# Two attention blocks on one core: the fifth product of the single-product pair placed ahead of the second

## The chip, the cores and the metric

The kernel runs on one core of a Trainium2 chip. The metric is the device time of one execution in microseconds. A core has a matrix engine (TensorE, in the profile PE for the matmuls and PEld for the loads of their stationary operand), three engines for elementwise work (VectorE or DVE, ScalarE or ACT, GpSimd or POOL) and a queue that issues transfers (SyncE or SP). Each engine works through its own list of instructions in order.[...]

## The reference

Two attention blocks follow one another on an input of 8 images, each 512 channels by 1024 positions, all in fp32:

```python
# block 0: 8 heads of 64 channels
h = group_norm(x, gn_weight, gn_bias)                       # 32 groups
qkv = jnp.einsum('oc,bct->bot', w_qkv, h.reshape(B, C, T)) + b_qkv[None, :, None]
weight = softmax(einsum('bct,bcs->bts', q * scale, k * scale))
a = jnp.einsum('bts,bcs->bct', weight, v).reshape(B, C, T)
x = x + (jnp.einsum('oc,bct->bot', w_proj, a) + b_proj[None, :, None]).reshape(B, C, H, W)
# block 1: one head of 512 channels
xn = group_norm(x, gamma, beta)                             # 8 groups
q, k, v = conv1x1(xn, q_w, q_b), conv1x1(xn, k_w, k_b), conv1x1(xn, v_w, v_b)
attn = softmax(einsum('bqc,bck->bqk', q, k) * C**-0.5)
x = x + conv1x1(einsum('bqk,bkc->bqc', attn, v), p_w, p_b)
```

Each projection ("convolution" in the kernel's words) is a product of a 512 x 512 weight matrix with a 512 x 1024 image.

## The kernel before, in words

The kernel goes through the 8 images one after another. For an image it makes values, keys and queries of block 0 (`values`, `keys_and_queries`), the attention of block 0 with its exponentials (`attention0`), the projection of block 0 (`projection2`), and for block 1 the product that stands for queries and keys together (`layer1_scores`, name g), the scores (`scores1`), the values with the projection folded in (name z) and their weighted sums (`values1`). Block 1 of one image stands between the attention and the values of block 0 of later ones.

**A twice divided convolution.** Most projections go through `conv2` (line 536). It uses a scheme of Strassen's kind: a product of matrices cut into 2 x 2 quarters is made from seven products of sums of quarters instead of eight. `conv2` does this twice, one level inside the other. The outer level has products 1 to 7. They are made in four pairs by `pair`: first pair 0 with the outer products 1 and 5, then pair 1 with 2 and 6, then pair 2 with the single product 7, and last pair 3 with 3 and 4. Pair 2 and pair 3 are interwoven. There are 44 such convolutions: v, k, q and p seven times each, g and z eight times each.

**The steps of one pair.** Inside a pair the inner level has seven products again, and `inner_steps` (line 452) sets their order. Each is a step: matmuls into one of three accumulation banks of PSUM called a, b and c, then an addition that takes the result away. `step(1)` fills bank a, and ScalarE copies it into bank b (line 482). Step 2 adds into a, steps 6, 7 and 4 add into b one after another, and steps 5 and 3 share bank c. The additions that empty them are:

- step 6: the sum in b is read into a small tile u2 (VectorE, `put`, line 468, which calls `add`, the profile's line 566); in pair 2 one addition that pair 1 left over (`flush`) follows it;
- step 2: the sum in a goes to the quarter (0,0) of the output;
- step 5: the content of c goes to a small tile c5;
- step 7: the sum in b plus c5 goes to the quarter (1,1);
- step 3: the content of c plus u2 goes to the quarter (0,1). Its first matmul starts the bank's second use: it adds onto what step 5 left there, so it may not run before the addition of step 5 has read c;
- step 4: the sum in b goes to the quarter (1,0).

For the single product of pair 2 GpSimd adds each finished quarter to other outputs (`extra`, which calls `more`, line 571): one addition when a quarter of `x` was read, one when the quarter was written, both after the VectorE addition of that step.

**The order around the change.** Each pair runs step 1, then what the pair before left for later (its steps 3 and 4 and its closing work, through `finish`), then a list of steps. Pair 2 also runs the first step of pair 3 inside its own list (`between`). Pair 3 then runs its own list, into which the steps 3 and 4 of pair 2 are set (`order`, where -3 and -4 stand for them). The order of the matmuls is the program's: the helper `matmul` (line 59) pins each of them. Most instructions on VectorE, ScalarE and GpSimd are not pinned to a place; a planner with costs of its own puts them in order per engine when the program is built, earliest ready first, in the program's order otherwise. Callables from a list of background work are run one per step (`run_background(1)`), and lists called `hooks` are run after the steps of a pair: in the convolution k the small matmuls of a group norm (`gvar`) follow step 7 of pair 2, in z the matmuls that add up the softmax's denominators (`sums`).

PSUM: during the convolutions each of the banks a, b and c has two buffers, so consecutive pairs alternate between them. The small tiles u2 and c5 have one buffer for even and one for odd pairs (line 177, `upool`).

Of the kernel before, what the change touches and what calls it, by code (L numbers as in the profile page):

```python
# [29 lines left out]
def two_attention_blocks_kernel(  # L30
# [143 lines left out]
    def main_path(ctx):  # L174
# [42 lines left out]
        def run_background(n):  # L217
            for _ in range(min(n, len(background))):
                background.pop(0)()
# [5 lines left out]
        def finish():  # L225
            while tail:
                tail.pop(0)()
# [135 lines left out]
        def image_factors(h, uid, sub=nc.vector.tensor_sub):  # L363

            tiles = [pair_tile(f"t{i}_{uid}") for i in (1, 2, 4)]
            halves = lambda t: (t[:, :HT], t[:, HT:])
            return right_sums(
                [halves(t) for t in h[:2]], [halves(t) for t in h[2:]],
                [lambda j, t=t: t[:, j, :] for t in tiles], sub,
            )  # L370
# [81 lines left out]
        def inner_steps(uid, parity, k, mm, add, y, x, extra, after7, final, early=(), defer=None, flush=None, between=(), order=None):  # L452

            ps, tmp = {}, {}

            def bank(n):
                ps[n] = ps_pools["abc".index(n)].tile([P, 2, 2 * P], F32, tag="ps", name=f"ps{n}_{uid}")[:, :k, :]

            def keep_tmp(what, tag):
                tmp[what] = upool.tile([P, 2, 2 * P], F32, tag=f"{tag}{parity}", name=f"{what}_{uid}")[:, :k, :]
                return tmp[what]

            def put(dst, n, at):

                if x is None:  # L470
                    (d,) = dst
                    nc.scalar.copy(d, ps[n])  # L472
                else:
                    add(dst, ps[n], x(*at))

            def step(j):
                if j == 1:
                    bank("a")
                    mm(ps["a"], 1, True)

                    bank("b")
                    nc.scalar.copy(ps["b"], ps["a"])  # L482
                elif j == 6:
                    mm(ps["b"], 6, False)
                    put([keep_tmp("u2", "u")], "b", (0, 1))
                    while flush:
                        flush.pop(0)()
                    extra(0, 1, True, False)
                elif j == 2:
                    mm(ps["a"], 2, False)  # L490
                    put(y(0, 0), "a", (0, 0))
                    extra(0, 0, True, True)
                elif j == 5:
                    bank("c")
                    mm(ps["c"], 5, True)
                    put([keep_tmp("c5", "w")], "c", (1, 1))
                    extra(1, 1, True, False)
                elif j == 7:
                    mm(ps["b"], 7, False)
                    add(y(1, 1), ps["b"], [tmp["c5"]])  # L500
                    extra(1, 1, False, True)
                elif j == 3:
                    mm(ps["c"], 3, False)
                    add(y(0, 1), ps["c"], [tmp["u2"]])
                    extra(0, 1, False, True)
                elif j == 4:
                    mm(ps["b"], 4, False)
                    if defer is None:
                        put(y(1, 0), "b", (1, 0))
                    else:  # L510
                        add(y(1, 0), ps["b"], x(1, 0), (0,))
                        defer.append(lambda: add(y(1, 0), ps["b"], x(1, 0), (1,)))
                    extra(1, 0, True, True)
                run_background(1)

            def run():
                if order is None:
                    step(1)
                    finish()
                    steps = [6, 2, *between, 5, 7]  # L520
                else:
                    three, four, *rest = tail
                    tail.clear()
                    steps = [{-3: three, -4: four}.get(j, j) for j in order] + rest
                for g in early:
                    g()
                for j in steps:
                    j() if callable(j) else step(j)
                for g in after7:
                    g()  # L530
                tail.extend([lambda: step(3), lambda: step(4)])
                tail.extend(final)

            return step, run
# [641 lines left out]
        for b in range(B):  # L1176
# [19 lines left out]
            af, steps = image_factors(a, f"a_{b}", here)  # L1196
# [68 lines left out]
        hf, steps = image_factors(h, f"h1_{B - 1}")  # L1265
# [206 lines left out]
```

## Time and profile before

| what | value |
|---|---|
| median of 3 runs | 2781.55 us (2780.86 to 2782.15) |
| the profiled execution | 2781.39 us |
| its span | 2779.6 us |
| TensorE matmuls, busy | 2764.8 us |
| VectorE, busy | 2052.0 us |
| GpSimd, busy | 1297.5 us |
| ScalarE, busy | 1000.3 us |
| granted TensorE clock | 1.000 |

Busy means that an instruction of the engine was under way. Matmuls overlap in the engine and the ends of their records are modelled, so that two matmuls started 0.22 us apart each have a record of 0.38 us. Whether TensorE lost time is therefore read from the starts of successive matmuls and not from the busy share. Each fp32 matmul of the source appears as two matmul instructions with 128 x 128 stationary values; the steps of the single-product pair have one source matmul with 256 columns (or two with 128 in the convolutions by tokens, v and z), the steps of the other pairs twice that. In the profile psa_g, psb_g and psc_g are the banks of convolution g, and so for the others; u_g is the tile u2, c_g the tile c5.

### The profile page before, as it was taken

The numbers are of one execution on the slowest core, as the hardware profiler recorded it, in microseconds if no ns is written. First come the engines' busy times: TensorE is split into PE (matmuls) and PEld (weight loads), VectorE is DVE, ScalarE is ACT, GpSimd is POOL, SyncE is SP. The second block draws the span as 40 slices with busy tenths as digits, with TensorE's granted clock in tenths as the row PEclk, the third lists the DMA queues.
The fourth block names the chain that finished last, engine by engine and source line by source line (L and its number), as shares of the span: only waits on it lengthen the run. The fifth ranks groups of instructions, "written<-read, shape, count | busy, mean of one in ns | idle before, by whom it ended". The sixth has DMA issues, their size and how long they took to land.

```text
span 2779.6 us, 36877 instructions
## 1 busy us (share of the span) xinstructions
PE 2764.8 (99%) x13436; PEld 1761.6 (63%) x13436; DVE 2052.0 (74%) x3214; ACT 1000.3 (36%) x1307; POOL 1297.5 (47%) x1384
## 2 busy tenths in 40 slices
PE   9999999999999999999999999999999999999999
PEld 6437636776376853868538694486844868338585
DVE  6587777777777777777786867777678776787776
ACT  1253463214632146312463125531255312633130
POOL 2313605745067440774307752176621766136763
PEclk9999999999999999999999999999999999999999
DMA  7827412344113440144401443014521145112302
GB/s 264 251 90 251 180 32 70 138 161 162 40 62 138 169 162 32 63 163 163 149 24 63 175 178 122 32 55 183 189 104 44 62 152 209 64 50 100 141 24 74
DMA packets 126070, 332.60 MB, mean 120 GB/s; under 512 B 19831, under 2 KB 64695, under 8 KB 114362
## 3 DMA queue, kind: packets, MB, share of 16 engines
q1 hardware_dynamic: 125294, 329.75, 33.3%
q8 instruction: 108, 1.77, 0.3%
q14 instruction: 80, 0.66, 0.1%
q10 hardware_dynamic: 588, 0.42, 0.0%
HBM read 258.14 MB, written 71.99 MB: 119 GB/s over the span
## 4 chain that ended last, share of the span: by engine, by line
PE 97%; DVE 2%; DMA 0%; issue 0%; ACT 0%; SPq 0%; DVEq 0%
PE sc L60 16%; PE av L60 16%; PE psb_av L60 5%; PE psb L60 5%; PE psa_av L60 4%; PE psc_av L60 4%; PE psc L60 4%; PE psa L60 3%; PE psb_k L60 3%; PE psb_z L60 3%; PE psb_q L60 3%; PE psb_p L60 3%; PE psb_g L60 3%; PE psb_v L60 3%; PE psc_v L60 2%; PE psc_p L60 2%
## 5 line engine op out<-in xcount | busy, mean ns | idle before, releaser
L700 DVE TENSOR_TENSOR sum<-sum,e 128x1024 f32<-128x1024 f32 x384 | 473.9, 1234 | 35.9 <-DVE sum L700 0.9
L696 ACT ACTIVATE e<-sc 128x1024 f32<-128x1024 f32 x512 | 476.1, 1050 | 63.4 <-PE sc L60 62.9
L60 PE MATMUL sc<-q,k 64*128 64x512 f32 x2048 | 456.8, 596 | 0.0
L60 PE MATMUL av<-e,v 128*64 128x512 f32 x2048 | 453.4, 595 | 0.0
L60 PEld LDWEIGHTS sc<-q,k 64*128 64x128 f32 x2048 | 190.1, 185 | 246.0 <-ACT e L696 120.9
L60 PEld LDWEIGHTS av<-e,v 128*64 128x64 f32 x2048 | 141.4, 137 | 299.0 <-issue 287.9
L434 POOL TENSOR_TENSOR inner_h<-x 128x256 f32<-128x256 f32 x16 | 14.8, 924 | 415.8 <-DVE x L1028 415.8
L698 DVE TENSOR_TENSOR sum<-e,e 128x1024 f32<-128x1024 f32 x64 | 79.9, 1249 | 103.9 <-ACT e L696 103.9
L719 ACT COPY a<-av 128x512 f32<-128x512 f32 x64 | 37.6, 587 | 318.7 <-PE av L60 279.2
L126 POOL TENSOR_TENSOR rstd<-ve,mhalf 128x4 f32<-128x4 f32 x16 | 16.7, 1042 | 274.5 <-DVE ve L124 274.5
L60 PE MATMUL psb<-inner,inner_h 128*128 128x256 f32 x448 | 115.6, 380 | 0.0
L60 PE MATMUL psa_av<-e,z 128*128 128x512 f32 x256 | 112.5, 592 | 0.0
L482 ACT COPY psb_v<-psa_v 128x512 f32<-128x512 f32 (+1 forms) x28 | 14.5, 517 | 234.0 <-DVE x L845 178.1
L60 PEld LDWEIGHTS psb<-inner,inner_h 128*128 128x128 f32 x448 | 84.5, 190 | 13.6 <-POOL inner L449 1.8
L60 PE MATMUL psb_z<-w_z,inner_h 128*128 128x128 f32 x672 | 87.5, 276 | 0.1
L60 PE MATMUL psb_g<-inner_h,w_m 128*128 128x256 f32 x336 | 84.9, 381 | 0.0
L776 ACT ACTIVATE e<-e 128x1024 f32<-128x1024 f32 x64 | 65.3, 1052 | 47.0 <-DVE e L766 25.7
L60 PEld LDWEIGHTS psb_z<-w_z,inner_h 128*128 128x128 f32 x672 | 81.4, 192 | 0.8 <-ACT u_z L472 0.3
L60 PEld LDWEIGHTS psa_av<-e,z 128*128 128x128 f32 x256 | 47.4, 190 | 53.6 <-issue 51.7
L771 POOL TENSOR_TENSOR e<-e,e 128x512 f32<-128x512 f32 x64 | 79.4, 1273 | 2.2 <-DVE e L766 2.1
L482 ACT COPY psb<-psa 128x512 f32<-128x512 f32 x56 | 31.9, 570 | 130.2 <-PE psa L60 130.2
L571 POOL TENSOR_TENSOR v<-v,v 128x256 f32<-128x256 f32 x28 | 20.4, 727 | 125.0 <-DVE u_v L566 121.8
(443 smaller groups left out, 6192.5 us busy)
## 6 DMA issues: line engine op xcount, KB each, us to landing
r<-all_rows SPq DMA_DIRECT2D x78, 256.0 KB
x<-in_x SPq DMA_DIRECT2D x36, 512.0 KB
h<-in_x SPq DMA_DIRECT2D x32, 512.0 KB
spill<-x SPq DMA_DIRECT2D x32, 512.0 KB
x<-spill SPq DMA_DIRECT2D x32, 512.0 KB
out<-x SPq DMA_DIRECT2D x63, 256.0 KB
kept<-a SPq DMA_DIRECT2D x28, 512.0 KB
again<-kept SPq DMA_DIRECT2D x28, 512.0 KB
```

Of the source, the lines that this page charges most:

```text
L60: tc.keep_in_program_order(nc.tensor.matmul(*args, **kw))
L126: nc.gpsimd.tensor_tensor(rstd, ve, mhalf, ALU.pow)
L434: pin(engine.tensor_tensor(dst, x, y, ALU.subtract))
L482: nc.scalar.copy(ps["b"], ps["a"])
L571: nc.gpsimd.tensor_tensor(d, x, y, ALU.add)
L696: nc.scalar.activation(e, sc, AF.Exp, scale=(C // 8) ** -0.5)
L698: nc.vector.tensor_add(total, es[0], e)
L700: nc.vector.tensor_add(total, total, e)
L719: nc.scalar.copy(dst, av)
L771: nc.gpsimd.tensor_tensor(blocks(dst, r, cc)[0], blocks(x, r, cc)[0], blocks(y, r, cc)[0], ALU.add)
L776: nc.scalar.activation(e[c, cc, r], e[c, cc, r], AF.Exp, scale=scale)
```

## The change

One line in `inner_steps` is different:

```diff
                 if order is None:
                     step(1)
                     finish()
-                    steps = [6, 2, *between, 5, 7]
+                    steps = [6, 5, *between, 2, 7] if between else [6, 2, 5, 7]
                 else:
                     three, four, *rest = tail
                     tail.clear()
```

Only pair 2 of a `conv2` has something in `between`, namely the first step of pair 3. With A for that step, the list of pair 2 was 6, 2, A, 5, 7 and becomes 6, 5, A, 2, 7. What follows is as it was: step 3 of pair 2, step 6 of pair 3, then step 4 of pair 2 and steps 2, 5 and 7 of pair 3 (in p: 5 of pair 3, 4 of pair 2, 7 and 2 of pair 3). The steps 5 and 2 change places together with their additions on VectorE and GpSimd. No instruction is added or removed, and no buffer changes.

## The prediction

> **What bounds the kernel now.** I read the page first: TensorE is busy for 99% of the span, and the chain that ended last is 97% TensorE.
>
> ```profile
> PE 2764.8 (99%) x13436; PEld 1761.6 (63%) x13436; DVE 2052.0 (74%) x3214; ACT 1000.3 (36%) x1307; POOL 1297.5 (47%) x1384
> ...
> PE 97%; DVE 2%; DMA 0%; issue 0%; ACT 0%; SPq 0%; DVEq 0%
> ```
>
> So a time saved on TensorE counts, unless another engine takes it back. Next I asked for the waits of TensorE's weight loader, because a stopped matmul shows first at the load in front of it:
>
> ```profile
> PEld psc_g L60 <- DVE c_g L566: 3.9, 8, 0.5
> ...
> PEld psc_q L60 <- DVE c_q L566: 3.4, 7, 0.5
> PEld psc_p L60 <- DVE c_p L566: 3.4, 7, 0.5
> ...
> PEld psb_k L60 <- DVE k L566: 2.3, 7, 0.3
> PEld psc_v L60 <- DVE c_v L566: 2.2, 8, 0.4
> ...
> PEld psc_k L60 <- DVE c_k L566: 0.5, 1, 0.5
> ```
>
> A wait of bank c for the tile c5 (total, times, longest), once per convolution: 8 times in g, 7 in q and p (v has one more elsewhere). The chain, cut out at one convolution g, shows that this wait is on the path:
>
> ```profile
> 1474.34 0.45 PE psc_g L60 x2
> 1474.78 0.02 issue
> 1474.81 0.43 DVE c_g L566
> 1475.24 0.04 issue
> 1475.29 0.70 PE psc_g L60 x2
> ```
>
> This is step 5 of pair 2, its addition into c5, and step 3 of pair 2. Only step 7 stands between. Its timeline:
>
> ```profile
> 1474.17 0.59 PE L60 MATMUL psc_g<-inner_h,w_m 128*128 128x256 f32 x2
> ...
> 1474.61 0.59 PE L60 MATMUL psb_g<-inner_h,w_m 128*128 128x256 f32 x2
> ...
> 1475.28 0.30 PEld L60 LDWEIGHTS psc_g<-x,w_m 128*128 128x128 f32 x2 [0.49 <-DVE c_g L566]
> 1475.29 0.70 PE L60 MATMUL psc_g<-x,w_m 128*128 128x256 f32 x2
> 1475.34 0.42 DVE L566 TENSOR_TENSOR g<-psb_g,c_g 128x256 f32<-128x256 f32 x1
> ...
> 1475.82 0.59 PE L60 MATMUL psb_g<-inner_h,w_m 128*128 128x256 f32 x2
> ```
>
> Steps 5, 7, 3 and the next step 6 begin at 1474.17, 1474.61, 1475.29 and 1475.82. At full pace a step of two matmuls takes 0.43 (5 to 7: 0.44). Step 7 to 3 takes 0.68, 0.25 too long: the wait. Step 3 to 6 takes 0.53, 0.10 too long: the load could not run ahead (the two matmuls have 0.70 instead of 0.59). Together 0.35 us per convolution. The starts of steps 5, 7, 3, 6 in q (1313.91, 1314.34, 1315.02, 1315.56) and p (1335.41, 1335.84, 1336.52, 1337.06) give the same, and one by one all 22 in g, q and p are within 0.002 of 0.353. In v (1270.25, 1270.70, 1271.38, 1271.93, a step there 0.447) it is (0.68 - 0.447) + (0.55 - 0.447) = 0.336.
>
> **What the Trainium skill says.** "Perfetto Trace Analysis", section Tensor Engine Instruction: the recorded end of a matmul is computed, and its semaphore goes out only when PSUM has acknowledged the write. Agreed: step 5's second matmul started at 1474.39 and its record ends at 1474.77; the addition starts at 1474.81. The same page, section Matmuls: independent groups should rotate through PSUM banks so that emptying one overlaps the next matmuls. Steps 5 and 3 accumulate in one bank, so here only the steps between them can cover the emptying. "TensorE: Matmul & The Clock Gate", section Step-by-step: loads are pulled ahead of running matmuls. Agreed: a load normally starts 0.21 before its matmul; after the wait both start together (1475.28, 1475.29), which is where the extra 0.10 comes from. "SBUF — State Buffer", section SBUF: two separate sides: VectorE and GpSimd share a port pair that one holds at a time. This case's trace agrees in k: a subtraction on two SBUF inputs takes 0.67 us in one place and 1.25 beside GpSimd additions.
>
> **The change part by part.** No instruction is added or removed, no transfer is issued or passed by a moved step (neither step 5 nor 2 issues one), and background work is run one piece per step as before.
>
> *Step 5 leaves its place before 7.* The chain from step 5's last start to step 3's load is 1474.39 to 1475.28, 0.89 us. Before, 0.43 us passed from that start until step 3's load was due (0.22 to the end of the matmul's turn, 0.43 of step 7, less the 0.21 by which a load runs ahead): 0.46 too little, of which the load's lead hides 0.21. After, A (four matmuls, 0.86), 2 and 7 (0.43 each) stand between: 1.72 in place of 0.43, so the chain ends 0.8 us before the load is due. The wait goes, and with it the refill: 0.35 in g, q, p, 0.336 in v. Step 5's factor is ready: step 6, which runs first, already needs the sum made after it. Its bank buffer and c5 were last used by pair 0.
>
> *Step 2 moves behind A.* Bank a of pair 2 isn't refilled in this convolution, so no matmul waits for its addition. Two things get later. On VectorE the addition of step 2 comes right before that of step 7: 1474.81 to 1475.23 in g, then step 7's to about 1475.7, at the time where it ends now. Step 4 needs that one (bank b), and comes 0.35 earlier: its load would be due at 1476.47 - 0.35 = 1476.12, some 0.4 after. No wait, but the cover shrinks from 0.7. On GpSimd the additions of step 2 follow that of step 5; the second one, which pair 3's step 2 needs, would end near 1476.8 in place of 1475.8 (each 0.73). That step's addition on VectorE starts at 1478.60 now, 1478.25 then: 1.4 us spare. GpSimd's last addition stays near 1479.75, as it waits in between; what uses it, the factors for the scores on GpSimd, has 1.0 us to spare, 0.6 then.
>
> *Step 6 of pair 3* needs ScalarE's copy of A: 1474.38 to 1474.95 in g, unmoved; its load will be due near 1475.25. Covered by 0.3.
>
> *z.* After step 7 come the 8 matmuls of `sums`; the c5 addition (1539.62 to 1540.04) is over when step 3's load starts at 1540.53. The remaining 0.2 there follows `sums` elsewhere too. Gain 0, though the wait view names c_z.
>
> *k.* Here the planner put a subtraction between the additions of steps 5 and 7, and step 4 waits for the latter:
>
> ```profile
> 1292.84 0.42 DVE L566 TENSOR_TENSOR c_k<-psc_k,k 128x256 f32<-128x256 f32 x1 [0.64 <-PE psc_k L60]
> ...
> 1293.18 1.25 DVE L168 TENSOR_TENSOR t_a<-again 128x512 f32<-128x512 f32 x1
> ...
> 1294.35 0.41 DVE L566 TENSOR_TENSOR k<-psb_k,c_k 128x256 f32<-128x256 f32 x1
> ...
> 1294.81 0.30 PEld L60 LDWEIGHTS psb_k<-inner_h,w_k 128*128 128x128 f32 x2 [0.34 <-DVE k L566]
> ```
>
> The stall before step 3 is about 0.27 (`gvar` covers a little), that before step 4 is 0.20. If the subtraction stays at the same time, step 3's gain is lost at step 4: 0. If it moves into the new pause after c5 or behind step 7's addition, both go: 0.47. If it lands before step 7's addition and delays GpSimd as well, k may lose up to 0.5. The trace doesn't show which; I take 0.15, between the ends, nearer to no gain because both ends of that stall hang on the same subtraction.
>
> **Sum.** 22 x 0.352 (g, q, p) = 7.74; v 7 x 0.336 = 2.35; k 7 x 0.15 = 1.05 (from -3.5 to 3.3); z 0. Together 11.1 us, against the profiled execution: 2781.39 - 11.1 = 2770.3 (span 2779.6 to 2768.5, 1.8 around it unchanged). The median of the runs lies 0.16 higher: 2770.4 us, 0.40% faster.
>
> **Rivals.** (1) *The wait moves to step 4.* Step 7's addition now queues behind step 2's, while step 4 comes earlier. If VectorE is 0.4 late in each convolution, the wait starts to return; 0.75 late, and all 0.35 is gone: about 2781, no change. Against it: in g, q, v and p no other VectorE work lies in the stretch from step 6 of pair 2 to step 4; for it: k shows the form. (2) *Only part arrives*: k loses 0.5 each, or the planner, whose order is made anew for the whole program, sets a few other instructions worse: 11.1 - 4.5 = 6.6 down to 5, so 2775 to 2776.5. (3) *More arrives*: k gives all, 13.4 in all: 2768.1. (4) *Slower: GpSimd holds up pair 3.* Its addition for step 2 of pair 3 waits on VectorE for GpSimd's additions of the moved step 2. They have 1.4 us to spare, and another 0.4 until step 3 of pair 3 needs the c5 addition queued behind. If GpSimd is 1.8 late, TensorE begins to wait; at 2.2 the gain is eaten; at 2.9 (four additions of 0.73 in front) each of 37 convolutions loses 1.1 - 0.35 = 0.75: +28 us, 2809. Against it: before pair 2, GpSimd idles 5.18 us in g, 19.9 in v, 15.7 in k, 4.4 in p; in q it is busy until then, yet its first addition starts 0.09 after u_q's end (1313.23 to 1313.32), as in g. That the change doesn't do what it says is excluded: matmuls are pinned, and only pair 2 has something between.
>
> **How the numbers follow.** The forecast with small variations of k (2768.8 to 2774): 0.65; more arrives, 2767 to 2768.8: 0.11; part arrives, 2774 to 2776.5: 0.12 (two thirds of it still over 0.2% faster); no change: 0.07; slower: 0.05. Two executions of this kernel differ by about 0.05%; I count 0.2% (5.6 us) as what a measurement can tell from no change. Faster: 0.65 + 0.11 + 0.08 = 0.84; same 0.11; slower 0.05. A range from 2767.3 to 2775.5 leaves out the slow cases and the extremes.
>
> **What would show it.** Right: no wait of psc_g, psc_q, psc_p or psc_v for c5, step 3 following step 7 after 0.43, and nothing new at step 4 or at pair 3. In k, the wait of psb_k for the addition of step 7 tells which case it is. Wrong: a wait of psb for step 7's addition in g, q, p or v (rival 1), or of VectorE for GpSimd before pair 3's step 2 (rival 4); or TensorE's gaps gone in the convolutions, and new ones in the attention.

## The result, and the profile after

The changed kernel takes 2768.3 us (median of 5 runs, 2767.79 to 2768.71), the kernel before 2782.0 beside it (5 runs, 2780.86 to 2782.76): a ratio of 0.9951, interval 0.9937 to 0.9966. The prediction was 2770.4 us in a range of 2767.3 to 2775.5. It had the right direction, and 2.1 us too little gain. The span of the profiled execution falls from 2779.6 to 2765.8 us, by 13.8, where 11.1 had been worked out.

The page of the changed kernel, engines and shares of the chain:

```profile
PE 2753.6 (100%) x13436; PEld 1762.1 (64%) x13436; DVE 2045.6 (74%) x3214; ACT 998.4 (36%) x1307; POOL 1291.4 (47%) x1384
...
PE 99%; DVE 1%; DMA 0%; issue 0%; SPq 0%; DVEq 0%
```

The instruction counts are those of before; VectorE's share of the chain went from 2% to 1%, as it should when the path no longer runs through its additions. The longest waits of the weight loader for VectorE and for ScalarE that are left in the convolutions (total, times, longest):

```profile
PEld psc_z L60 <- DVE z L566: 3.3, 8, 0.4
...
PEld psb_g L60 <- ACT psb_g L482: 2.5, 6, 0.4
```

The lines with 3.9, 3.4, 3.4 and 2.3 us of before are gone, and of the 2.2 of psc_v one wait of 0.4 is left, elsewhere. The wait for ScalarE's copy is unchanged (2.5 us, 6 times, before as well). The chain, in the same pair of a convolution g:

```profile
1465.33 0.43 PE psc_g L60 x2
1465.76 1.29 PE psa_g L60 x6
1467.05 0.43 PE psb_g L60 x2
1467.48 0.43 PE psc_g L60 x2
```

Step 5 at 1465.33, then A and step 2 as one entry of six matmuls in bank a (1.29 = 0.86 + 0.43), step 7 and step 3. Every entry starts when the one before it ends at full pace. The 0.43 of "DVE c_g" that stood in this chain before, with 0.02 and 0.04 of issue, has no successor. The timeline of the same stretch shows where the additions went:

```profile
1466.04 0.41 DVE L566 TENSOR_TENSOR c_g<-psc_g,g 128x256 f32<-128x256 f32 x1
...
1466.66 0.57 ACT L482 COPY psb_g<-psa_g 128x512 f32<-128x512 f32 x1 [0.47 <-PE psa_g L60]
...
1467.09 0.42 DVE L566 TENSOR_TENSOR g<-psa_g,g 128x256 f32<-128x256 f32 x1 [0.64 <-PE psa_g L60]
...
1467.32 0.59 PE L60 MATMUL psc_g<-x,w_m 128*128 128x256 f32 x2
...
1467.52 0.42 DVE L566 TENSOR_TENSOR g<-psb_g,c_g 128x256 f32<-128x256 f32 x1
1467.54 0.84 PEld L60 LDWEIGHTS psb_g<-inner_h,w_m 128*128 128x128 f32 x4
```

The c5 addition is over at 1466.45, and step 3 starts at 1467.32, its load 0.21 before: 0.66 us from the addition's end to the load, where before the load stood waiting and followed after 0.05 (1475.23 to 1475.28). The addition itself starts later behind its step than before, 0.66 us after step 5's last matmul start (1465.38) and not 0.42, because on VectorE it now follows the two additions of step 6 directly. ScalarE's copy of A ends at 1467.23, 0.31 ahead of the load of step 6 of pair 3 (1467.54). The additions of steps 2 and 7 follow one another, as said.

To put the 13.8 us in places, I took all matmul starts of the convolutions and subtracted from each distance the full-pace one (0.216 us for 256 columns, 0.112 for 128). What is left over is stall. Summed by convolution and step, after against before:

| convolution | change of stall, us | where |
|---|---|---|
| g, q, p (22) | -2.82, -2.47, -2.47: -7.76 | step 3 of pair 2 |
| v (7) | -2.82 | step 3 of pair 2 -2.34; a single stall of one v at step 5 of pair 0 -0.73; step 7 of pair 3 +0.26 |
| k (7) | -2.49 | step 3 of pair 2 -1.13, step 4 -1.37 |
| z (8) | -0.23 | none at step 3 of pair 2; step 7 of pair 0 -0.27 |
| sum | -13.31 | |

(Small entries are left out, so the parts of a row need not add up exactly.) The other 0.5 of the span's 13.8 lies outside the convolutions. By the starts the stalls there fell by 0.8: 0.3 at the beginning of the run, where transposes wait for raw weights, and 0.5 at the matmuls of the scores and of the denominators. The stretches before the first matmul and after the last are together 0.3 longer. In the eight experiments below that add nothing on GpSimd the sum of the stalls outside lies between -1.0 and +0.7 us against before, so I count it to no theory.

The attention gives nothing back: the gain collects evenly, 0.32 to 0.36 us per convolution that had the stall (0.55 in the last k, which has no `gvar` at that place).

In k the prediction had left open where the subtraction `t_a` would land. The timeline of one k in the changed kernel:

```profile
1286.15 0.42 DVE L566 TENSOR_TENSOR k<-psa_k,k 128x256 f32<-128x256 f32 x1 [0.64 <-PE psa_k L60]
1286.49 0.68 DVE L168 TENSOR_TENSOR t_a<-again 128x512 f32<-128x512 f32 x1
1286.72 1.04 POOL L571 TENSOR_TENSOR k<-k,k 128x256 f32<-128x256 f32 x1 [0.38 <-DVE k L566]
...
1287.09 0.42 DVE L566 TENSOR_TENSOR k<-psb_k,c_k 128x256 f32<-128x256 f32 x1
```

and the lines of the kernel before that belong beside the prediction's fence of k:

```profile
1293.15 0.73 POOL L571 TENSOR_TENSOR k<-k 128x256 f32<-128x256 f32 x1
...
1295.08 0.67 DVE L168 TENSOR_TENSOR t_a<-again 128x512 f32<-128x512 f32 x1
1295.09 1.26 POOL L571 TENSOR_TENSOR k<-k 128x256 f32<-128x256 f32 x1
```

The subtraction stayed where it was, ahead of step 7's addition: counted from the start of step 6 of pair 2 it starts 2.70 us later in both kernels. But it lasts 0.68 us instead of 1.25. Before, a GpSimd addition had started 0.03 ahead of it (1293.15 against 1293.18). Now GpSimd's addition waits for the later addition of step 2 and starts 0.23 behind it (1286.72 against 1286.49), and it is GpSimd's that takes longer, 1.04 instead of 0.73. In all seven k it is so. The next subtraction of the same k had shown this order already in the kernel before: it starts 0.01 us ahead of a GpSimd addition and takes 0.67, and the addition takes 1.26.

### The profile page after: what moved, and what is told of

Read it like the earlier page. It is cut to its first block, busy times and chain, and to the rows that moved or that the text cites. A ratio compares the mean times of both kernels' runs of the same rounds, so it can differ in the third digit from the quotient of the medians.

```text
span 2765.8 us, 36809 instructions
## 1 busy us (share of the span) xinstructions
PE 2753.6 (100%) x13436; PEld 1762.1 (64%) x13436; DVE 2045.6 (74%) x3214; ACT 998.4 (36%) x1307; POOL 1291.4 (47%) x1384
## 4 chain that ended last, share of the span: by engine, by line
PE 99%; DVE 1%; DMA 0%; issue 0%; SPq 0%; DVEq 0%
PE sc L60 16%; PE av L60 16%; PE psb_av L60 6%; PE psb L60 5%; PE psa_av L60 4%; PE psc_av L60 4%; PE psc L60 4%; PE psa L60 3%; PE psb_v L60 3%; PE psb_k L60 3%; PE psb_p L60 3%; PE psb_q L60 3%; PE psb_g L60 3%; PE psb_z L60 3%; PE psc_z L60 2%; PE psa_k L60 2%
## 5 line engine op out<-in xcount | busy, mean ns | idle before, releaser
L820 POOL TENSOR_TENSOR t<-e,t 128x1024 f32<-128x1024 f32 x32 | 78.4, 2482 | 0.0
```

The costliest lines, as they stand in the source:

```text
L820: on = lambda *a: lambda: tc.keep_in_program_order(nc.gpsimd.tensor_tensor(*a))
```

## The experiments

What each adds to or takes from the kernel before stands as a diff of the list of steps. None leaves out any of the computation; those with extra instructions write results that nothing reads. Expected numbers are the texts on record.

**1. Step 5 alone is moved.** Does the whole gain come from moving 5 ahead of A, with the move of 2 behind A free?

```
-                    steps = [6, 2, *between, 5, 7]
+                    steps = [6, 2, 5, *between, 7]
```

> The list of pair 2 is 6, 2, 5, A, 7: step 5 moves ahead of A, step 2 keeps its old place. Theory A (only the distance of step 5 from step 3 counts): A and 7 stand between, 1.29 us of matmuls, so step 3's load is due 1.30 after step 5's last start and the chain needs 0.89. No wait for c5, about 2768.5 us (2767.5 to 2770), span near 2766. Theory B (what helped is that step 2's additions came later, out of the way of step 5's on VectorE and GpSimd): the wait stays, about 2781.5 us.

Measured: 2771.9 us (2771.06 to 2774.06), ratio 0.9967, interval 0.9953 to 0.9981; span 2770.4, 4.6 longer than the change's. The wait for c5 is gone in all 36 places, as in the change: -2.82, -2.47, -2.47 and -2.35 in g, q, p and v, and k's two stalls too. But a new stall stands at step 6 of pair 3, which adds into the bank that ScalarE's copy of A fills: 0.13 us each in g and p, 0.06 in q, 0.09 in v, in sum 3.0. The timeline of a g:

```profile
1469.51 0.57 ACT L482 COPY psb_g<-psa_g 128x512 f32<-128x512 f32 x1 [0.91 <-PE psa_g L60]
...
1469.74 0.59 PE L60 MATMUL psc_g<-x,w_m 128*128 128x256 f32 x2
...
1470.20 0.94 PEld L60 LDWEIGHTS psb_g<-inner_h,w_m 128*128 128x128 f32 x5 [0.26 <-issue]
1470.23 1.10 PE L60 MATMUL psb_g<-inner_h,w_m 128*128 128x256 f32 x4
```

The copy ends at 1470.08, step 3 has started at 1469.74, so step 6 was due at 1470.17, its load 0.21 before. The load comes at 1470.20, 0.12 after the copy's end, and the matmul starts 0.06 late. The next load could not run ahead in the meantime, so the second matmul follows after 0.29 instead of 0.216; the others keep full pace. Only steps 7 and 3, 0.86 us, stand between A and step 6 here; in the kernel before it was 5, 7 and 3, and in the change 2, 7 and 3. So the move of step 2 isn't idle: it puts back the cover that step 5 takes away from A's copy. I had not seen this ahead of the run. The rest of the 4.6 us lies in z and outside the convolutions (0.3 and 1.3 by the starts), where the kernels differ from one another anyway.

**2. Step 2 alone is moved.**

```
-                    steps = [6, 2, *between, 5, 7]
+                    steps = [6, *between, 2, 5, 7]
```

> The list of pair 2 is 6, A, 2, 5, 7: step 2 moves behind A, step 5 keeps its distance of one step from step 3. Theory A: the wait for c5 stays at 0.35 us in each g, q, p and v, about 2781.5 us (2780 to 2783). Theory B: the gain is here too, about 2768.5 us.

Measured: 2780.15 us (2778.85 to 2780.82), ratio 0.9995 (0.9986 to 1.0004): the same as before. Waits of the weight loader:

```profile
PEld psc_g L60 <- DVE c_g L566: 3.9, 8, 0.5
...
PEld psb_k L60 <- DVE k L566: 1.1, 7, 0.2
```

The c5 wait stays whole, since step 5 still has only step 7 behind it. Alone in k something goes: 1.19 us at step 4, where the subtraction takes 1.07 instead of 1.24. With experiment 1 this gives the division: step 5 ahead of A pays, step 2 behind A by itself pays next to nothing, and only both keep what 5 brings.

**3. A behind everything.** If the copy's cover is the term, a kernel that leaves only step 3 between A and step 6 must lose more than it gains.

```
-                    steps = [6, 2, *between, 5, 7]
+                    steps = [6, 2, 5, 7, *between]
```

> The list of pair 2 is 6, 2, 5, 7, A: step 3 is covered by 7 and A (1.29 us), but only step 3 now stands between A and step 6 of pair 3, which needs ScalarE's copy of A. Theory A with the same sum for this wait: A's last start to the end of the copy and the semaphore 1.03 us (0.42, 0.57, 0.05), the load due after 0.44, so 0.59 late, of which the load's lead hides 0.21; plus 0.10 for the refill: 0.48 us in each of 36 convolutions (z has the sums in between: 0 to 0.1). No wait for c5, a wait of psb for ScalarE's copy, about 2768.3 + 17.5 = 2785.8 us (2783 to 2788), slower than before. A theory that only c5 matters expects 2768.5.

Measured: 2786.33 us (2785.5 to 2788.03), ratio 1.0017 (1.0011 to 1.0024). The stall at step 6 of pair 3 is 0.56 in g and p, 0.49 in q, 0.54 in v, 0.30 in k. Waits:

```profile
PEld psb_q L60 <- ACT psb_q L482: 4.4, 7, 0.6
```

The c5 wait is gone here too (-2.82, -2.47, -2.46, -2.35), and what it gave is eaten. So the covers behind A order as the arithmetic wants: three steps of 0.43, no stall; two, some 0.1 (none in k); one, some 0.5 (0.30 in k). From two to one it grows by just the 0.43 of the step that is missing. The expectation of 0.48 took 0.05 us from the copy's end to the load. That holds in q; in g, p and v the load starts 0.11 to 0.12 after it, here as in experiment 1, and g and p lose 0.06 more than q. What holds the load there is open.

**4. The change in k alone.** It separates k's share from the rest.

```
-                    steps = [6, 2, *between, 5, 7]
+                    steps = [6, 5, *between, 2, 7] if between and uid[0] == "k" else [6, 2, *between, 5, 7]
```

> The new list in the convolution k alone, the old one in v, q, p, g and z. By the matmuls' starts k lost 2.49 us of waits in the changed kernel (1.12 before step 3, 1.37 before step 4), so theory A expects 2779.4 us against 2781.9 before, a span near 2777.1, and in k no wait for c5 and none before step 4. If the second wait of k went because of what other convolutions do, it stays: a span near 2778.5.

Measured: 2778.66 us (2777.92 to 2779.9), ratio 0.9991 (0.9982 to 1.0); span 2776.9. The ratio's interval reaches 1, so the time by itself doesn't show k's share; the stalls do. In k they fall by 2.49, the same as in the change (-1.13 and -1.37), and g, q, p and v keep theirs (within 0.1 us of before). The subtraction lasts 0.68 in all seven k. What k gives is thus the own effect of the list in k, and not of another instruction order elsewhere in the program.

**5 to 7. The first rival, in three sizes.** Would the wait move to step 4 if VectorE were later? Between the additions of steps 2 and 7 come one, two or three copies of bank a (128x256, VectorE, to a tile that nobody reads):

```
+            def late():
+                for i in range(1):          # 1, 2 or 3
+                    t = upool.tile([P, 2 * P], F32, tag=f"late{i}", name=f"late{i}_{uid}")
+                    nc.vector.tensor_copy(t, ps["a"][:, 0, :])
...
-                    steps = [6, 2, *between, 5, 7]
+                    steps = [6, 5, *between, 2, late, 7] if between else [6, 2, 5, 7]
```

One copy:

> The changed kernel with one more VectorE instruction in pair 2, between the additions of steps 2 and 7: a copy of bank a, 128x256, into a tile nobody reads (0.35 to 0.42 us). In the changed kernel step 7's addition in g ends at 1467.94 and step 4's load starts at 1468.40: 0.41 spare after the semaphore. Theory A (a wait is the lateness beyond the cover): at most 0.1 us in some convolutions, 2768.3 to 2771 us. A theory that each VectorE instruction in this stretch is paid for expects 36 x 0.38 = 14 us more, 2782.

Two copies:

> The same with two such copies: step 7's addition comes 0.7 to 0.8 later, 0.3 to 0.4 beyond the cover. Theory A: step 4's load is that much late, its lead hides 0.21 of it, plus 0.10 for the refill: 0.2 to 0.3 us in g, q, v and k (29 convolutions; p has step 5 of pair 3 in between, z the sums), 6 to 9 us: about 2775.5 us (2772 to 2779). My rival 1 in the prediction left the load's lead out and would give 0.3 to 0.5, 9 to 14 us: 2777 to 2783.

Three copies:

> The changed kernel with three copies between the additions of steps 2 and 7. With two, step 7's addition came 0.58 later than without (copies follow one another after 0.335), and step 4 lost only 0.05. If a stall is the lateness beyond the cover (0.41) less the load's lead (0.21), plus 0.10 for the refill, three copies put it 0.92 late: 0.92 - 0.41 - 0.21 + 0.10 = 0.40 us in each of g, q and k, some 0.3 in v, about 11 us, 2779 us (2776 to 2781), and a wait of psb for step 7's addition in nearly all of them. If VectorE's lateness does not reach step 4 at all, as two copies alone could suggest: 2771.

Measured: 2767.56 us with one (2767.34 to 2768.22; ratio 0.9951), 2770.16 with two (2769.69 to 2770.53; 0.9959), 2777.94 with three (2777.24 to 2780.05; 0.9989, interval 0.9980 to 0.9998). The stall at step 4 in g is 0, 0.05 and 0.38 us, in q 0, 0.05 and 0.38, with three copies also 0.32 in v and 0.19 in k. With two copies, in g:

```profile
1469.23 0.42 DVE L566 TENSOR_TENSOR g<-psa_g,g 128x256 f32<-128x256 f32 x1 [0.64 <-PE psa_g L60]
1469.57 0.74 DVE L456 COPY late_g<-psa_g 128x256 f32<-128x256 f32 x2
1470.24 0.41 DVE L566 TENSOR_TENSOR g<-psb_g,c_g 128x256 f32<-128x256 f32 x1
```

and the weight loader's wait in g with three:

```profile
PEld psb_g L60 <- DVE g L566: 4.1, 8, 0.5
```

Two copies put step 7's addition 1.01 us behind step 2's (1469.23 to 1470.24), where the change has 0.43 (1467.09 to 1467.52): 0.58 late. The expectation had taken two copies for more, by their single durations; on the engine they follow at about 0.335 each. That is why two copies missed their number and three were run: 0.58 + 0.335 = 0.92 late by the sum, 0.90 in the trace (1472.31 to 1473.64 in a g). Against a cover of 0.41 and the load's lead of 0.21 (the time by which a load starts ahead of its matmul) 0.92 leaves 0.30, and with the 0.10 that is lost while the loads get ahead again (the refill) 0.40; measured 0.38. With two copies 0.58 - 0.41 = 0.17 is less than the lead, and nearly nothing is seen (0.05). So the mechanism of rival 1 exists, but it begins to cost at some 0.6 us of lateness, and the change leaves step 4 without a wait.

**8. The fourth rival, brought about.** Four GpSimd additions (128x256) ahead of those of the moved step 2.

```
+            def late():
+                for i in range(4 if between else 0):
+                    (d,) = y(0, 0)
+                    t = upool.tile([P, 1, 2 * P], F32, tag=f"late{i}", name=f"late{i}_{uid}")
+                    nc.gpsimd.tensor_tensor(t, d, d, ALU.add)
...
-                    put(y(0, 0), "a", (0, 0))
+                    put(y(0, 0), "a", (0, 0)); late()
...
-                    steps = [6, 2, *between, 5, 7]
+                    steps = [6, 5, *between, 2, 7] if between else [6, 2, 5, 7]
```

> The changed kernel with four more GpSimd additions, 128x256 (0.73 us each), ahead of those of step 2 in pair 2, their results unused: the additions that step 2 of pair 3 waits for end 2.9 us later. By rival 4 of the prediction 1.8 us of that is covered, so each of g, q, v and k loses 1.1 us less what GpSimd's own pauses take in: 36 x 0.5 to 1.1 = 18 to 40 us, 2786 to 2808, with waits of VectorE for GpSimd before pair 3's step 2. If GpSimd's pauses take in all of it: 2768.5.

Measured: 2817.27 us (2816.25 to 2818.28), ratio 1.013 (1.0113 to 1.0147). Waits of the weight loader:

```profile
PEld psc_k L60 <- DVE c_k L566: 10.6, 7, 1.7
...
PEld psb L60 <- POOL inner L449: 9.2, 15, 0.9
...
PEld psc_g L60 <- DVE c_g L566: 8.0, 8, 1.0
...
PEld psb_p L60 <- POOL inner_a L434: 4.9, 7, 0.7
```

In the chain of causes that the rival named, pair 3's addition waits for GpSimd, and behind it on VectorE stands the addition into c5 of pair 3, for which step 3 of pair 3 waits: stalls of 0.87 us in g, 1.33 in q, 1.38 in k, 0.54 in v, in sum 29.8. (The expectation's 36 counts too many: g, q, v and k are 29 convolutions, and z loses nothing there.) More places come in that the rival left out, above all two: the factors that GpSimd makes next are late (`inner_a` before p, 0.57 each; `inner` for the scores, 9.2 us of the weight loader's time over 15 waits). In the changed kernel the weight loader waits neither for the c5 of k or g nor for `inner_a`, and for `inner` 2.1 us over 7 waits, where it was 1.8 over 6 before: GpSimd is not late in it. But the price of it being late is higher than I had put it.

**9. Step 7 ahead of step 2.** The list that gives the addition of step 7 its old place.

```
-                    steps = [6, 2, *between, 5, 7]
+                    steps = [6, 5, *between, 7, 2] if between else [6, 2, 5, 7]
```

> The list of pair 2 is 6, 5, A, 7, 2: step 5 covered by A, 7 and 2, step 6 of pair 3 covered by 7, 2 and 3 as in the change, and step 7's addition one place earlier, so that step 4 has more cover. If the two covers (1.29 us of matmuls or more behind step 5 and behind A) are all that counts, the same time as the change: 2768.3 us (2767 to 2769.5). If the later step 2 now holds up pair 3 through GpSimd, slower by up to 0.1 us in each convolution: 2769.5 to 2772.

Measured: 2769.14 us (2768.97 to 2770.33), ratio 0.9958 (0.9941 to 0.9974): the same as the change within the intervals. Pairs 2 and 3 have lost the same stalls, step for step (g -2.82, q -2.47, p -2.47, v -2.34, k -1.13 and -1.37). The small difference is a single wait elsewhere:

```profile
PEld psc_v L60 <- DVE x L845: 1.3, 1, 1.3
```

That is one v out of seven, at the same position that in the change had 0.73 less than before. No list tried beats the change by more than its interval.

## Why the prediction was right, and where it was short

*What bounds the kernel, and the 0.35.* Right, by term. The wait of 0.25 and the 0.10 of refill were both in the starts, and both went: 7.76 us in g, q and p against 7.74 worked out, 2.34 in v's step 3 against 2.35. The chain is covered by A, 2 and 7, but with 0.6 us to spare and not the 0.8 worked out. The prediction kept the chain at 0.89; it takes 1.13, since the c5 addition now queues behind step 6's two (0.66 to its start, 0.42, and 0.05 to the load).

*z at 0.* Right at the place in question: the stall before step 3 of pair 2 (some 2.4 us in sum over the 8, by the matmul starts) stays in every kernel. The weight loader's wait there is still put down to VectorE (before to c_z, 2.3 us in 6 waits, now to z, 3.3 in 8, in the fence above), but the matmuls lose neither more nor less: `sums` covers the additions, as the prediction had it.

*k at 0.15.* This is the term that was mis-sized: 1.05 us in the sum, 2.49 measured, alone and in the whole change. The step that failed is "If the subtraction stays at the same time, step 3's gain is lost at step 4: 0." It did stay at the same time. But its length of 1.25 was no constant: it held GpSimd's time as well. The prediction had both durations (0.67 and 1.25) and named the Trainium skill's reason ("SBUF — State Buffer", section SBUF: two separate sides: a VectorE instruction with two SBUF inputs and a GpSimd instruction that reads SBUF exclude each other, and whichever starts first holds the ports for its whole instruction). But it read only the longer one as standing beside GpSimd additions, where both do (1295.08 and 1295.09 above), and did not ask which of the two would be first once GpSimd's additions move. The two instructions share no tile, and yet one sets the other's length. The traces agree with that rule: the subtraction takes 1.24 us when a GpSimd addition of 0.73 has started 0.03 ahead of it (before), 1.17 when 0.10 ahead (six of seven in experiment 1), 1.07 when 0.20 ahead (experiment 2), and 0.68 when that addition is all but over, 0.63 ahead (experiment 3), or starts after it (the change, k alone); in the change GpSimd's addition pays instead. Its length alone doesn't make the stall: in experiment 1 it starts at 1.97 after step 6 instead of 2.70, with one copy (experiment 5) it stands behind step 7's addition and takes 1.21 in six of seven, and both times step 4 loses nothing. No run varied only the start of the GpSimd addition, so this cause is read from the order of the starts in these kernels, not isolated.

*The rest of the gap.* The span gained 2.7 us more than worked out. k is 1.44 of it. One v's own wait and what goes with it is 0.47, z's step 7 of pair 0 with the small entries 0.23, and 0.5 lies outside the convolutions: 2.6. Only k is tied to the change by a run of its own. The others come and go with other lists too: against before, the wait of that v lies between -0.73 and +0.64 in the experiments without work on GpSimd, z's between -0.28 and 0.

*Step 2 behind A.* "No matmul waits for its addition" and the shrunken cover of step 4 held: no wait at step 4 in g, q, p and v. Yet the prediction took this move for a pure cost to be bounded, and the cover of A's copy ("covered by 0.3") for a thing untouched. Both numbers were right (0.31 in the change), but the reason wasn't seen: the 0.3 survives because step 2 comes in for step 5. Without it, new stalls of 3.0 us in sum stand at that place (experiment 1).

*The rivals.* More arrives (3), which the prediction gave a chance of 0.11, was the case that came, at 2768.1 against 2768.3, though not by its sum, so that the closeness is in part luck: k gives all but the 0.13 us each that `gvar` keeps before step 3 (2.49 of its 3.3), and the odd places above make up the rest. The wait at step 4 (1) was priced without the load's lead, so it starts near 0.6 us of lateness and not at 0.4 (0.05 lost at 0.58). GpSimd (4) was priced at 2809 for four additions; four cost 2817. Its own term was counted for 37 convolutions, z among them, and came in 29 (29.8 us); what GpSimd makes after the pair was not counted. Its threshold was not measured.

## What to carry to other kernels

In an in-order stream of matmuls the price of a wait can be worked out from four times. Here it is the chain (last matmul start to the load that may follow, 0.89 us) less the time until that load was due (0.43), less the lead by which loads run ahead of their matmuls (0.21), plus the refill (0.10): 0.35. All four can be read from starts in one timeline, and the chain has to be read anew for the new order, as the additions on VectorE change places too. When a step is moved away from a wait, ask also which other waits it had been covering, and let a step of the same length take its place, as the swap does here and the single move doesn't. When an addition moves, look at what runs beside it on VectorE and GpSimd: an instruction's length there can change without the instruction being touched.

## What the runs showed of the hardware

- The same VectorE subtraction (128x512, two SBUF inputs) takes 0.68 us when it starts ahead of a GpSimd addition and 1.07 to 1.25 when it starts 0.20 to 0.03 us behind one: the closer behind, the longer. The loser ends about 0.55 to 0.6 us after the winner: 1293.15 + 0.73 = 1293.88 to 1293.18 + 1.25 = 1294.43 before; 1286.49 + 0.68 = 1287.17 to 1286.72 + 1.04 = 1287.76 after.
- Small VectorE instructions that read PSUM follow each other faster than their recorded lengths: two copies record 0.74 together, and each sets the next one back by about 0.335.
- The lead of the weight load hides the first 0.2 us of a late result: 0.17 us of lateness beyond the cover cost 0.05 (two copies), 0.49 cost 0.38 (three: 0.90 less 0.41).
